# An S4D macaron block in fp32 on one core: ACT and DVE in program order from the 14th to the 49th group

## The chip, the core and the metric

One NeuronCore of a Trainium2 chip runs the whole program. The time is device microseconds (us) of one execution; lower is better. The kernel before was run three times: 1751.17 us in the median, 1746.32 and 1751.95 us at the ends.

## The reference, cut to what matters

Input x is 8 x 2048 x 256 (batch, length, channels), fp32. Three residual sublayers follow each other:

```python
x = x + 0.5 * ffn(layernorm(x), w1, b1, w2, b2)     # first half, "a"
x = x + s4d(layernorm(x), ...)                      # state-space layer, then a layer norm of its own
x = x + 0.5 * ffn(layernorm(x), w1, b1, w2, b2)     # second half, "b"

def ffn(x, w1, b1, w2, b2):
    h = relu(x @ w1 + b1)                           # 256 -> 1024
    return h @ w2 + b2                              # 1024 -> 256

def s4d(x, ...):                                    # a long convolution along the length, per channel
    K = 2 * real(sum_n Ct[h, n] * exp(dtA[h, n] * l))
    y = irfft(rfft(x, 4096) * rfft(K, 4096))[:2048]
    r = x + y + x * D
    return layernorm(r) * ln_w + ln_b
```

## The kernel before, in words

**Stages.** The convolution is made in blocks of 128 positions. It needs tables that follow from the state-space parameters alone: for every pair of channels a matrix of powers called P, and its transpose. The tables are made by the vector engines while the first FFN runs; then come the states and outputs of the convolution, then the second FFN.

**The FFN.** Every fp32 product is made of three fp32r products of high and low parts. Tokens are handled in 64 groups of 256. A group has 8 slots of the loop variable `t` in `sublayer`, one for each 128 hidden features; slot 23.4 is the fourth slot of group 23, t = 188. In a slot TensorE makes the hidden features `ph_a` (`up`, L857, six matmuls) and, three slots later (`LAG = 3`), multiplies the hidden parts `hx_a` into `po_a` (`down`, L867, six matmuls). Between them ACT makes the high part with a relu (L946) and DVE the low part (L116, `SCALAR_TENSOR_TENSOR hx_a`). PSUM holds four `ph` banks.

**Around a group.** `pre_a` loads a group (`xa`, issued from ACT's queue at L1012), takes its moments on DVE (L675, L679), normalizes on ACT (`xn`, L726), adds the bias on GpSimd (POOL, L773, pinned behind what was traced on POOL before it), turns it on TensorE (`pt_a`, L790) and splits it (ACT `xh_a` L799, DVE `xl_a` L801). `post_a` adds the result (L1023), takes moments, and writes the next layer's normalized input `u` (ACT, L726). The root and the reciprocals of a finished group are shared with a group to come: `s_u` on ACT (L686), `t_u`, `q_u`, `nb_u` on DVE (L697, L119, L708).

**The background: P.** `matrices` is a generator that `fill` advances beside the groups; each `yield` carries a pace in us that `fill` weighs against 1.32 us a slot. P is made in 32 batches:
- `make` (POOL, L599, L601, L603, L605, L607, L609): six operations of 128 x 512 into one of four areas of `u` for batches 0 to 15 (an area is used again by the batch four later), and into another set of areas for 16 to 31. L601 to L609 pass through one scratch tile, so the last four of a batch follow each other. Batch 16's scratch and area lie over tables that batches 0 to 7 read.
- `spread`: two copies on ACT (L618, `planes<-u`) split P into 16-bit halves, then SyncE's queue issues a transposing DMA (L620, `planes<-planes`) and a store (L625, `o<-u`).
- `transpose`: one copy on DVE and one on ACT (L635, `u<-planes`) put the halves together, and SyncE's queue stores them (L637, `pt<-u`). After that the area is free.

There is one buffer each for `planes` and `turned`, so the copies of a batch wait until the transposing DMA of the batch before has read them. The copies L618, L635 and the DMA L620 are pinned (`keep_in_program_order`) behind the instruction traced before them on their engine. In the program the two L618 copies of batch 6 stand in slots 21.6 and 21.7, of batch 8 in 23.4 and 23.5, of batch 9 in 24.3 and 24.4, of batch 12 in 26.7 and 27.0; the copies L635 of a batch come some 8 or 9 slots after its first L618. `lags` makes another table beside it: L535, L537, L541 on POOL, `pk` on TensorE (L549), two DVE operations, and DMAs issued by POOL (L569). The first L618 copy stands in slot 16.5, the last L635 copies in 46.2.

**What sets the order.** The program is traced in the order of the Python code. Then a scheduler orders each engine's instructions by a simulated timeline, within the data dependencies and the pins. Each engine's queue then runs in the order so fixed, and an instruction that waits holds up all behind it. `tc.manual_schedule(engines=...)` takes ACT and DVE out of the scheduler's hands for what is traced inside it: they keep the order of the code. The kernel before uses it for the slots before t = 0 alone.

Of the kernel before, what the change touches and what calls it, by code (L numbers as in the profile page):

```python
# [43 lines left out]
def macaron_s4d_kernel(  # L44
# [35 lines left out]
    XL = 8  # L80
    LAGS_BEHIND = 3
    PIN = 1
    PINF = "a1", "a2"
    MB = 1
    PINT = 1
# [23 lines left out]
    def bank(tag, name):  # L109
        return ps.tile([P, 512], F32, name=name, tag=tag, bufs=BANKS[tag])  # L110

    def slot(tag, shape, name, dtype=F32):
        return work.tile(shape, dtype, name=name, tag=tag, bufs=BUFS[tag])

    def stt(o, a, s, b, op0, op1):
        return V.scalar_tensor_tensor(out=o, in0=a, scalar=s, in1=b, op0=op0, op1=op1)  # L116
# [554 lines left out]
    def stats(srcs, name, pin=False, mv=None):  # L671
        st = stat.tile([P, NTB, 6], F32, name=f"st_{name}", tag="st")
        mv = moments(NTB, name) if mv is None else mv
        for i, src in enumerate(srcs):
            ins = V.bn_stats(st[:, i, :], src)  # L675
            if pin:
                tc.keep_in_program_order(ins)
        for i in range(NTB):
            V.bn_aggr(mv[:, i, :], st[:, i, :])  # L679
        return mv  # L680
# [64 lines left out]
    def halves(xt):  # L745
        return [xt[:, i, :] for i in range(NTB)]

    def ffn_in(xt, name, on_act=NTB, by_dma=False, joint=None, into=None):
# [7 lines left out]
        else:  # L756
            mv = stats(halves(xt), f"f{name}", name in PINF)
            yield
# [92 lines left out]
    def up(wt, xT, ph, fc):  # L851
        xh, xl = xT
        fs = slice(fc * P, (fc + 1) * P)
        n = 0
        for dc in range(NDC):
            for wp, xp in ((1, xh), (0, xl), (0, xh)):
                nc.tensor.matmul(  # L857
                    ph, wt[wp][:, dc, fs], xp[dc] if type(xp) is list else xp[:, dc, :], start=(n == 0), stop=(n == 3 * NDC - 1)
                )
                n += 1  # L860

    def down(wt, hs, po, fc):
        hh, hl = hs
        for i in range(NTB):
            tsl = slice(i * P, (i + 1) * P)
            for n, (hp, wp) in enumerate(((hl, 0), (hh, 1), (hh, 0))):
                nc.tensor.matmul(  # L867
                    po[:, i, :],
                    hp[:, tsl],
                    wt[wp][:, fc, :],  # L870
                    start=(fc == 0 and i == 0 and n == 0),
                    stop=(fc == NFC - 1 and n == 2),
                    skip_group_check=True,
                )

    def sublayer(w1t, w2t, pre, post, lead, tag, first=(), background=(), due=(), at=(), wide=None):

        xT, po, running = {}, {}, {}
        background = iter(background)
        due = dict(due)
        at = dict(at)
        now = [0.0, 0.0]
        last = {}

        def step():  # L890
            while spawned:
                key, what = spawned.pop(0)
                running["later", key] = what
            for key in list(running):
                try:
                    next(running[key])
                except StopIteration as e:
                    del running[key]
                    if key[0] == "pre":
                        xT[key[1]] = e.value  # L900

        def fill(until=None):
            while until or now[1] <= now[0]:
                pace = next(background, "end")
                if isinstance(pace, str):
                    due.pop(pace, None)
                    if pace == "end":
                        now[1] = math.inf
                    if pace in (until, "end"):
                        return  # L910
                else:
                    now[1] += pace

        W0, W1 = (wide.first, wide.end) if wide else (NG, NG)
        starts_at = {}
        for g in range(NG):
            sooner = wide.sooner(g) if wide else 0
            starts_at.setdefault(g * SLOTS - lead - sooner, []).append(g)

        ordered = ExitStack()  # L920
        if first or tag == "b" and MB:
            ordered.enter_context(
                tc.manual_schedule(engines={mybir.EngineType.Activation, mybir.EngineType.DVE})
            )
        for t in range(-lead, NG * SLOTS + LAG + 1):
            if t == 0:
                ordered.close()
            g, k, f = t // SLOTS, t % SLOTS // 2, t % 2
            if W0 <= g < W1:
                g0, fc = g // 2 * 2, (t - g // 2 * 2 * SLOTS) // 2  # L930
                if f == 0:
                    hx = wide.hidden()
                    for i in range(2):
                        pend[g0 + i, fc] = [h[:, i * TOK : (i + 1) * TOK] for h in hx]
                    ph = bank("h", f"ph_{tag}{g0}_{fc}")
                    up(w1t, wide.input(g0), ph, fc)
                    last[A_] = A_.activation(hx[0], ph, AF.Relu)  # L937
                    last[V] = stt(hx[1], ph, 0.0, hx[0].bitcast(F32), ALU.max, ALU.subtract)
            elif t >= 0 and g < NG:
                fc = 2 * k + f  # L940
                hx = slot("hx", [P, 2, TOK], f"hx_{tag}{g}_{fc}", F32R)
                hh, hl = pend[g, fc] = hx[:, 0], hx[:, 1]
                ph = bank("h", f"ph_{tag}{g}_{fc}")[:, 0:TOK]
                up(w1t, xT[g], ph, fc)

                last[A_] = A_.activation(hh, ph, AF.Relu)  # L946
                last[V] = stt(hl, ph, 0.0, hh.bitcast(F32), ALU.max, ALU.subtract)
            tb = t - LAG
            tw = t - WLAG
            if W0 * SLOTS <= tw < W1 * SLOTS:  # L950
                g0 = tw // (2 * SLOTS) * 2
                fc, i = divmod(tw - g0 * SLOTS, 2)
                if fc == 0:
                    po[g0 + i] = wide.result(f"po_{tag}{g0 + i}").rearrange("p (i m) -> p i m", i=NTB)
                down(w2t, pend.pop((g0 + i, fc)), po[g0 + i], fc)
                if fc == NFC - 1:
                    running["post", g0 + i] = post(g0 + i, po.pop(g0 + i))
            if 0 <= tb < NG * SLOTS and not W0 * SLOTS <= tb < W1 * SLOTS:
                gb, fc = tb // SLOTS, tb % SLOTS
                if tb % SLOTS == 0:  # L960
                    po[gb] = bank("o", f"po_{tag}{gb}").rearrange("p (i m) -> p i m", i=NTB)
                down(w2t, pend.pop((gb, fc)), po[gb], fc)
                for mark in [m for m, d in due.items() if d == gb]:
                    fill(mark)
                if tb % SLOTS == SLOTS - 1:
                    running["post", gb] = post(gb, po.pop(gb))
            for n in starts_at.get(t, ()):
                running["pre", n] = pre(n)
            if t == -lead:
                running["first"] = iter(first)  # L970
            step()
            if t >= 0:
                now[0] += 1.32
                with ExitStack() as behind:
                    for ins in last.values():
                        behind.enter_context(tc.issue_after(ins.ins))
                    fill()
            if t in at:
                at[t]()
        while running:  # L980
            step()
        fill("end")
# [285 lines left out]
    def begin():  # L1268
        for _ in range(sizes[1] // PB):
            next(head)  # L1270

    sublayer(
        w1t, w2t, pre_a, post_a, 19, "a", load_weights(), chain(matrices(), early()),
        {"half": NG // 2, "tables": NG * 3 // 4},
# [123 lines left out]
    def pre_b(g):  # L1398
# [8 lines left out]
        uc = [uo[:, i // CQ, :, i % CQ] for i in range(P - 1 - i0, P - 1 - i0 - NTB, -1)]  # L1407
        mv = stats(uc, f"r{g}", PIN & 2)
        yield
# [9 lines left out]
        for i in range(NTB):  # L1419
            xb = xt[:, i, :].rearrange("p (b h) -> p b h", h=BCH)  # L1420
            ins = stt(xb, uc[i], rs[:, i : i + 1], xb, ALU.mult, ALU.add)
            if PIN & 1:
                tc.keep_in_program_order(ins)
# [4 lines left out]
    def post_b(g, po):  # L1428
# [7 lines left out]
        )  # L1436

    sublayer(
        [wb1[:, i] for i in range(2)], [wb2[:, i] for i in range(2)], pre_b, post_b, 17, "b",
        wide=wide,  # L1440
# [33 lines left out]
```

## Time and profile before

| what | number |
|---|---|
| median of three runs | 1751.17 us (1746.32 to 1751.95) |
| the profiled execution | 1747.17 us, of which the span is 1745.3 us |
| busy over the span | TensorE matmul 1713.1, DVE 1368.3, ACT 968.4, POOL 586.3 us |
| mean granted TensorE clock | 0.994 |
| groups 14 to 48 | 183 to 618 us of the span |
| in these 435 us | TensorE busy 428.26, DVE 320.45, ACT 312.53, POOL 309.20 us |

In the profile PE is TensorE's matmuls and PEld its weight loads, SPq is SyncE's queue of DMA issues, and ACTq is ACT's. Times in timelines count from the start of the span. "Idle before" is the time in which an engine stood still ahead of an instruction, with what ended it.

### The profile page before, as it was taken

What the parts mean: (1) busy time and instruction counts of PE and PEld (TensorE: products, weight loads), DVE (VectorE), ACT (ScalarE), POOL (GpSimd) and SP (SyncE); (2) the same over time, 40 slices, a digit from 0 to 9 for tenths busy, and PEclk for the clock granted to TensorE, in tenths of its full rate; (3) what the DMA queues carried; (4) which work ended last, traced back from release to release, by engine and by line L of the source; (5) the groups of instructions that cost most, each with busy time, mean ns of one, the idle gap of its engine ahead of it and who ended that gap; (6) DMA issues with size and microseconds to landing.
All of it is one profiled execution on the core that took longest, in us unless ns stands there. A gap on an engine that the chain in (4) does not pass through costs nothing.

```text
span 1745.3 us, 38327 instructions
## 1 busy us (share of the span) xinstructions
PE 1713.1 (98%) x14263; PEld 1638.1 (94%) x14263; DVE 1368.3 (78%) x4591; ACT 968.4 (55%) x2040; POOL 586.3 (34%) x550
## 2 busy tenths in 40 slices
PE   9999999999999999999999899999999999999998
PEld 7999999989999999999999799999999999999998
DVE  6998776677777767766999788889888788788754
ACT  4555477677778755544555445555455455445533
POOL 1117989886776105111000132231222222222200
PEclk9999999999999999999999989999999999999999
DMA  5111166577666532236888912332223323222211
GB/s 191 47 40 53 49 178 164 160 199 205 188 167 190 134 85 68 73 91 194 263 259 260 292 49 72 70 90 56 67 73 73 73 67 79 73 67 73 63 48 37
DMA packets 276849, 204.24 MB, mean 117 GB/s; under 512 B 162740, under 2 KB 235188, under 8 KB 276150
## 3 DMA queue, kind: packets, MB, share of 16 engines
q1 hardware_dynamic: 249232, 168.08, 36.2%
q10 hardware_dynamic: 26502, 32.52, 5.9%
q8 instruction: 112, 1.84, 0.4%
q0 software_dynamic: 928, 1.19, 0.3%
q14 instruction: 75, 0.61, 0.1%
HBM read 91.89 MB, written 71.57 MB: 94 GB/s over the span
## 4 chain that ended last, share of the span: by engine, by line
PE 80%; DVE 12%; DMA 4%; issue 1%; ACT 1%; SPq 0%; POOL 0%; ACTq 0%; DVEq 0%
PE po_b L867 21%; PE ph_b L857 20%; PE po_a L867 19%; PE ph_a L857 18%; DVE e L1160 2%; DMA planes<-planes 2%; DVE te L1161 2%; DVE xsB L1163 1%; DVE xsA L1163 1%; PE pt_a L790 1%; DVE xsA L1162 1%; DVE xsB L1162 1%; DMA xa<-in_L_attn_x_dram 1%; DMA wb<-w_dram 1%; PE pv L1130 1%
## 5 line engine op out<-in xcount | busy, mean ns | idle before, releaser
L867 PE MATMUL po_a<-wa,hx_a 128*128 128x256 f32 x3072 | 454.7, 285 | 6.8 <-DVE hx_a L116 6.6
L857 PE MATMUL ph_a<-xh_a,wa 128*128 128x256 f32 x2048 | 456.4, 287 | 1.2 <-ACT xh_a L799 0.7
L867 PEld LDWEIGHTS po_a<-wa,hx_a 128*128 128x128 f32 x3072 | 405.3, 192 | 9.5 <-DVE hx_a L116 8.0
L857 PEld LDWEIGHTS ph_a<-xh_a,wa 128*128 128x128 f32 x2048 | 355.3, 193 | 4.3 <-ACT wa L194 1.5
L946 ACT ACTIVATE hx_a<-ph_a 128x256 fp32r<-128x256 f32 x512 | 193.8, 388 | 229.5 <-PE ph_a L857 207.4
L116 DVE SCALAR_TENSOR_TENSOR hx_a<-ph_a,hx_a 128x256 fp32r<-128x256 f32 x512 | 209.0, 414 | 121.8 <-ACT hx_a L946 119.8
L867 PEld LDWEIGHTS po_b<-wb,hb 128*128 128x128 f32 x2208 | 288.1, 191 | 14.4
L867 PE MATMUL po_b<-wb,hb 128*128 128x256 f32 x2208 | 292.6, 282 | 0.0
L857 PE MATMUL ph_a<-xl_a,wa 128*128 128x256 f32 x1024 | 290.3, 285 | 0.0
L857 PE MATMUL ph_b<-xh_b,wb 128*128 128x256 f32 (+1 forms) x928 | 249.8, 327 | 0.7 <-ACT xh_b L799 0.7
L937 ACT ACTIVATE hb<-ph_b 128x512 fp32r<-128x512 f32 x184 | 109.2, 594 | 162.1 <-PE ph_b L857 161.2
L857 PEld LDWEIGHTS ph_a<-xl_a,wa 128*128 128x128 f32 x1024 | 197.4, 193 | 0.6 <-DVE xl_a L801 0.4
L116 DVE SCALAR_TENSOR_TENSOR hb<-ph_b,hb 128x512 fp32r<-128x512 f32 x184 | 124.9, 679 | 83.3 <-ACT hb L937 81.0
L773 POOL TENSOR_TENSOR xa<-xa,hb 128x512 f32<-128x512 f32 x64 | 85.1, 1330 | 286.9 <-ACT xn L726 245.9
L857 PEld LDWEIGHTS ph_b<-xh_b,wb 128*128 128x128 f32 x928 | 167.3, 193 | 12.8 <-ACT xh_b L799 1.1
L857 PE MATMUL ph_b<-xl_b,wb 128*128 128x256 f32 (+1 forms) x464 | 151.1, 327 | 0.0
L857 PE MATMUL ph_b<-even,wb 128*128 128x512 f32 x576 | 149.0, 393 | 0.0
L867 PE MATMUL po_b<-wb,hx_b 128*128 128x256 f32 x864 | 126.5, 285 | 3.9 <-DVE hx_b L116 3.9
L867 PEld LDWEIGHTS po_b<-wb,hx_b 128*128 128x128 f32 x864 | 114.2, 193 | 4.8 <-DVE hx_b L116 4.5
L857 PEld LDWEIGHTS ph_b<-even,wb 128*128 128x128 f32 x576 | 102.4, 189 | 16.9
L773 POOL TENSOR_TENSOR u<-u,hb 128x512 f32<-128x512 f32 x32 | 46.4, 1449 | 177.0 <-ACT xn L726 144.6
L946 ACT ACTIVATE hx_b<-ph_b 128x256 fp32r<-128x256 f32 x144 | 54.0, 381 | 73.0 <-PE ph_b L857 67.9
(292 smaller groups left out, 3028.4 us busy)
## 6 DMA issues: line engine op xcount, KB each, us to landing
o<-u SPq DMA_DIRECT2D x32, 512.0 KB, 4.0
pt<-u SPq DMA_DIRECT2D x32, 512.0 KB, 4.0
tz<-kpad SPq DMA_DIRECT2D x64, 256.0 KB, 4.5
x_dram<-xa ACTq DMA_DIRECT2D x62, 256.0 KB, 2.1
xa<-in_L_attn_x_dram ACTq DMA_DIRECT2D x61, 256.0 KB, 3.0
pt<-pt SPq DMA_DIRECT2D x60, 256.0 KB, 3.7
ot<-o SPq DMA_DIRECT2D x48, 256.0 KB, 4.1
u<-x_dram SPq DMA_DIRECT2D x32, 256.0 KB, 2.8
```

The source lines that it names most:

```text
L116: return V.scalar_tensor_tensor(out=o, in0=a, scalar=s, in1=b, op0=op0, op1=op1)
L773: return G_.tensor_add(xt, xt, hb2.unsqueeze(1).to_broadcast([P, NTB, H]))
L790: nc.tensor.transpose(pt[:, dc * TOK + i * P : dc * TOK + (i + 1) * P], xn[:, i, dc * P : (dc + 1) * P], ident,)
L857: nc.tensor.matmul(ph, wt[wp][:, dc, fs], xp[dc] if type(xp) is list else xp[:, dc, :], start=(n == 0), stop=(n == 3 * NDC - 1))
L867: nc.tensor.matmul(po[:, i, :], hp[:, tsl], wt[wp][:, fc, :], start=(fc == 0 and i == 0 and n == 0), stop=(fc == NFC - 1 and n == 2), skip ...
L937: last[A_] = A_.activation(hx[0], ph, AF.Relu)
L946: last[A_] = A_.activation(hh, ph, AF.Relu)
L1130: ins = nc.tensor.matmul(pv[ri][c * N : (c + 1) * N, l, j0 * B : j1 * B], pts[c][:, l, ri * N : (ri + 1) * N], some(j0, j1)[:, :, BCH * bt ...
L1160: E.tensor_mul(t1, xv[:, :, :, j, :], wr_b)
L1161: E.tensor_mul(t2, xv[:, ::-1, :, j, :], wi_b)
L1162: E.tensor_add(xv[:, :, :, j + 1, :], xv[:, :, :, j + 1, :], t1)
L1163: E.tensor_add(xv[:, :, :, j + 1, :], xv[:, :, :, j + 1, :], t2)
```

## The change

Two places: a pair of slots, and a block in the loop of `sublayer` that opens `manual_schedule` for ACT and DVE at the start of the 14th group of the first FFN and closes it at the start of the 49th. What lies inside, the background included, keeps the order of the code on these two engines. No instruction is added, removed or altered; POOL, TensorE and SyncE stay with the scheduler.

```diff
@@ -80,6 +80,7 @@
     PIN = 1
+    IN_ORDER = 14 * 8, 49 * 8
     PINF = "a1", "a2"
@@ -925,6 +926,14 @@
         for t in range(-lead, NG * SLOTS + LAG + 1):
             if t == 0:
                 ordered.close()
+
+            if tag == "a" and t in IN_ORDER:
+                if t == IN_ORDER[0]:
+                    ordered.enter_context(
+                        tc.manual_schedule(engines={mybir.EngineType.Activation, mybir.EngineType.DVE})
+                    )
+                else:
+                    ordered.close()
             g, k, f = t // SLOTS, t % SLOTS // 2, t % 2
```

## The prediction

> **What bounds the kernel now.** First the page: the busy shares, and the rows of its slices for TensorE, POOL and the clock (a slice is 43.6 us).
>
> ```profile
> PE 1713.1 (98%) x14263; PEld 1638.1 (94%) x14263; DVE 1368.3 (78%) x4591; ACT 968.4 (55%) x2040; POOL 586.3 (34%) x550
> PE   9999999999999999999999899999999999999998
> POOL 1117989886776105111000132231222222222200
> ```
>
> TensorE bounds the program, so the change is worth what it does to TensorE's idle time between 183 and 618 us, where groups 14 to 48 lie. POOL is busy 80 to 90% in the slices from 175 to 400 us: there P is made. Next, busy time by stretches of 10 us (columns: PE, PEld, DVE, ACT, POOL, clock, DMA share, GB/s):
>
> ```profile
> 325.00:335.00 10.00, 10.00 (x88) 10.00 (x87) 5.40 (x21) 4.71 (x10) 9.37 (x9) 1.00 0.52 122
> 335.00:345.00 10.00, 8.15 (x56) 7.95 (x55) 6.61 (x18) 7.14 (x12) 3.17 (x3) 0.83 0.63 194
> 345.00:355.00 10.00, 9.08 (x75) 8.84 (x74) 5.66 (x20) 7.00 (x13) 9.99 (x11) 1.00 0.91 209
> 385.00:395.00 10.00, 7.14 (x60) 6.94 (x59) 6.96 (x27) 6.88 (x13) 8.69 (x8) 1.00 1.10 283
> ```
>
> All the loss sits in a few stretches: 56 matmuls instead of 86 to 88, then 75, then 60. TensorE's idle time before single instructions from 183 to 618 us is 1.85 us at 340.10, 0.92 at 354.83, 0.36 at 356.88, 2.86 at 392.93 and 0.56 at 563.67; with some shorter gaps 6.74 us. In the clock record one period of 3.41 us from 340.14 us stands at 0.5, which is 1.7 us of work. Together 8.4 us: more than this the change can't bring. Then the timelines of the three engines around the first stall:
>
> ```profile
> 327.44 1.99 ACT L618 COPY planes<-u 128x1024 uint16<-128x1024 uint16 x2
> 332.09 0.38 ACT L946 ACTIVATE hx_a<-ph_a 128x256 fp32r<-128x256 f32 x1 [1.31 <-PE ph_a L857]
> 336.13 1.99 ACT L618 COPY planes<-u 128x1024 uint16<-128x1024 uint16 x2 [3.65 <-DMA planes<-planes]
> ...
> 332.85 0.17 DVE L708 RECIPROCAL t_u<-q_u 128x4 f32<-128x4 f32 x1
> 336.15 1.30 DVE L635 COPY u<-planes 128x1024 uint16<-128x1024 uint16 x1 [3.13 <-DMA planes<-planes]
> ...
> 337.97 0.28 PE L857 MATMUL ph_a<-xh_a,wa 128*128 128x256 f32 x1
> 340.10 1.65 PE L867 MATMUL po_a<-wa,hx_a 128*128 128x256 f32 x6 [1.85 <-DVE hx_a L116]
> ```
>
> The copies at 327.44 are batch 8's, those at 336.13 batch 9's. Between them lie 8.7 us, and batch 8's transposing DMA took 6.6 us of these (329.45 to 336.0). Both engines stand at the front of their queues for that DMA, with relus and low parts behind them; TensorE runs dry. In the code the two batches' copies are seven slots apart. They came so close because batch 8 was late: its copies follow the relu of slot 23.4, which ended at 305.70, and 32 later instructions of ACT were let past them. POOL shows why:
>
> ```profile
> 289.77 1.06 POOL L599 TENSOR_TENSOR u<-u 128x512 f32<-128x512 f32 x1 [2.03 <-DVE mv_j L679]
> 290.79 1.06 POOL L605 TENSOR_TENSOR u<-u 128x512 f32<-128x512 f32 x1
> 291.81 1.28 POOL L609 TENSOR_TENSOR u<-u 128x512 f32<-128x512 f32 x1
> ...
> 296.81 1.28 POOL L609 TENSOR_TENSOR u<-u 128x512 f32<-128x512 f32 x1
> ...
> 322.11 1.29 POOL L609 TENSOR_TENSOR u<-u 128x512 f32<-128x512 f32 x1
> ```
>
> L609 ends a batch: 6 at 293.1, 7 at 298.1, 8 only at 323.4. At 289.77 POOL starts batch 9 before it has ended batch 6, and idles for that. Between 298.1 and 323.4 it does batch 8's last four operations (4.9 us), all that is left of batch 16 (6.0), L541, L535 and L537 (4.6), three bias additions (3.9), the starts of batches 10 and 11 (4.2) and DMA issues (2.1).
>
> **The change part by part.** No operation changes; what moves is the order. I laid the trace's rows against the code. Of ACT's instructions from group 32 to 48, 63 of 331 stand elsewhere than in the code, by at most four places, and TensorE idles 0.56 us there: for ACT the order of the code nearly ran there already. In groups 22 to 31 it is 179 of 194, up to 32 places. So ACT's change falls between 270 and 410 us. On DVE most instructions move by a few places everywhere.
>
> *TensorE's cushion.* A slot is six `ph` and six `po` matmuls, 0.72 us each six. From the end of `ph` of a slot to the `po` that needs its `hx` lie three of each, 4.3 us. The relu (0.38), the low part (0.41) and two handovers of 0.1 take 0.9 or 1.0 of it. ACT or DVE may be 3.4 us late at no cost; beyond that TensorE waits one for one, once, since all later slots shift with it.
>
> *What goes: up to 8.4 us.* The stalls at 340, 355 and 393 us come from batches that crowd. In the code's order they stay seven slots (10 us) apart, more than one DMA (median 4.7, longest 7.5 us from issue to landing) and its copies. The 8.4 us can go.
>
> *What comes: ACT waits for POOL.* Copies that are not ready now hold up ACT itself: queued behind them are the relus, and DVE's low parts and TensorE wait for those. The price is how late L609 is behind the relu ahead of the copies, less 3.4 us. POOL can't keep its order: what needs a copy that stands behind the waiting one can't run ahead of it any more.
> - Batch 6: the relu of slot 21.6 ended at 281.10. L607 of batch 6 ended at 287.7. Batch 9's start needs the area of batch 5, whose L635 copies stand in slot 22.0, behind the waiting ones, so it can't come in between; L609 then ends at 289.0 or sooner. That is 289.0 - 281.1 - 3.4 = 4.5 us at most. Without batch 8's start (2.1) and L535, L537 (1.2), which the code has later, it is 285.7, and 1.2 us.
> - Batch 8: 305.7 + 3.4 = 309.1. POOL free at 298.1, own four operations 4.9, one bias addition 1.3: 304.3, no stall. If all of the trace's work stays in between except what can't (batch 11's start and the bias of group 25, 3.4 us), L609 ends at 320.0: 10.9 us.
> I take 2.0 us for both together, 1.2 to 10.9. It is nearer the lower end, because the rows of batches 7, 9 and 10 show the last four operations back to back, about 5 us, and what was done for batch 6 or 8 is a stall paid once.
>
> *What comes: bursts.* In the order of the code each relu waits for all of the slot before. I added the slots' work on ACT and DVE by start-to-start distances (relu 0.27, low part 0.33, `planes` copy 0.95, `u` 0.65 us) against 1.44 us a slot: one place exceeds the cushion, group 15, by 0.5 us (table work beside 13 small operations of `q_u`, `nb_u`). Taken by full durations, which overlap in the trace, the same sum gives far more, so I keep 0 to 3 us, and take 0.5: groups 32 to 48 lose next to nothing.
>
> *DVE's copies beside POOL.* L635 on DVE took 0.73 to 3.12 us, on ACT 1.32 to 1.42. At its worst 2.4 us over the shortest, it stays under the cushion: nothing. The Trainium skill (SBUF — State Buffer, "Who interferes with whom") says that a DVE copy in a two-port mode and a GpSimd operation exclude each other for a whole instruction, which speaks against a fixed order on DVE beside a busy POOL. By that page the excess is one POOL operation, an estimate of 1.3 us, again nothing in the sum.
>
> *The clock.* An idle gap of 1.85 us came with a period of 3.41 us at half clock, one of 2.86 us with none. So a new stall costs 0 or 1.7 us more; I take 0. The Trainium skill (TensorE: Matmul & The Clock Gate, "What's actually happening") has the clock fall after an idle window of about 3.4 us, free-running; by that alone no stall of 2 us would pay, and the row at 340 shows one that did.
>
> Outside the stretch the order is the scheduler's again; I put it at nothing, as TensorE hides it there as before (98%).
>
> Sum: 8.4 - 2.0 - 0.5 = 5.9 us less. The profiled execution took 1747.17 us (span 1745.3 and 1.9 around it), 4.0 under the median of the runs; against the median 1751.2 - 5.9 = 1745.3 us. The forecast's own ends: 8.4 less, or 8.4 - 4.5 - 3.0 = 0.9 less: 1742.8 to 1750.3.
>
> **The rivals.**
> - *Slower: POOL becomes the bound.* One place, batch 8: if POOL still does batch 16 and the rest first, ACT stands 10.9 us. It decides as soon as that batch's L609 ends later than 305.7 + 3.4 + 8.4 = 317.5 on the trace's scale. Later batches add at most what is left of batch 12's lateness (L609 at 369.8, the relu ahead of it at 349.9): 369.8 - 349.9 - 10.9 - 3.4 = 5.6. With 0.5 for bursts and 1.7 for the clock, 10.9 + 5.6 + 2.2 - 8.4 = 10.3 us more, 1761.5. For: POOL is busy 90% from 200 to 340 us. Against: much of that is work for later batches, and an ACT that waits serves POOL's results at once instead of 4 us after.
> - *No change: the loss moves.* Batches 6 and 8 together cost 5 to 8 us, in place of the crowding: 8.4 - 6.5 - 0.5 = 1.4 us less, 1749.8. For: POOL has the same work. Against: its idle time ahead of batch 9 (2.03 us) goes.
>
> **How the numbers follow.** What a measurement of this kernel can tell from no change is 0.3%, 5.3 us. The forecast gets 0.45, the slower rival 0.28, the other 0.27. The range goes from 1739, as single runs lie 5 us under the median, to 1762, the slower rival's sum; outside I leave some 0.15.
>
> **What would show it.** Right: no gap of PE at `po_a` over 1 us between 330 and 400 us, L618 copies seven slots apart and their waits on POOL (L609) rather than on the DMA, 2 to 5 us in all; PE busy 432 of 435 us. Wrong: ACT idle for 10 us or more before `planes` L618 with L609 as the releaser, relus behind it, PE idle there; or gaps at low parts spread over all groups, which would be the bursts.

## The result: slower by 1.4%

The changed kernel took 1774.78 us in the median of four runs (1773.86 to 1780.26), the kernel before 1751.56 us beside it: ratio 1.0144, 95% interval 1.0123 to 1.0165. The prediction was 1745.3 us, with a range from 1739 to 1762. It was wrong in sign.

The page of the changed kernel's profile (span 1773.3 us, before 1745.3), busy shares and the slices of TensorE and POOL:

```profile
PE 1722.3 (97%) x14263; PEld 1643.3 (93%) x14263; DVE 1375.0 (78%) x4591; ACT 965.8 (54%) x2040; POOL 586.0 (33%) x550
PE   9999999899999999999999979999999999999998
POOL 1117988974676113211000032231222222222210
```

The work is the same; the span is 28.0 us longer. Where these 28.0 us were lost is read best by laying the two traces beside each other, slot by slot. For the first slot of each group I take the start of the relu, after less before, and how much that grows from one group to a later one. TensorE's idle time and the time lost at half clock in the same groups stand beside it (both us; a half-clock period of 3.4 us counts as 1.7):

| groups | growth | TensorE idle, before → after | lost at half clock, before → after |
|---|---|---|---|
| 14 to 20 | +7.1 | 0.0 → 4.7 | 0.0 → 1.7 |
| 20 to 33 | +12.0 | 6.2 → 14.3 | 1.7 → 6.8 |
| 33 to 42 | +0.1 | 0.0 → 0.0 | 0.0 → 0.0 |
| 42 to 50 | +11.4 | 0.6 → 7.7 | 0.0 → 0.0 |
| 50 to the end | -2.7 | | |

So there are three losses, and a calm stretch in which the order of the code costs nothing at all. Stretches of the changed kernel, columns as in the prediction (PE, PEld, DVE, ACT, POOL, clock, DMA share, GB/s):

```profile
205.00:215.00 10.00, 6.05 (x38) 5.85 (x38) 8.51 (x21) 2.06 (x6) 9.04 (x11) 0.83 0.10 29
320.00:330.00 10.00, 7.78 (x52) 7.79 (x53) 7.40 (x29) 8.38 (x16) 9.84 (x12) 0.83 0.87 201
335.00:345.00 10.00, 6.40 (x35) 6.40 (x36) 5.47 (x21) 6.76 (x13) 9.45 (x9) 0.66 0.61 170
560.00:570.00 10.00, 7.64 (x63) 7.29 (x62) 8.23 (x31) 6.44 (x13) 7.94 (x7) 1.00 0.47 105
```

Before, a slice of 10 us lost its matmuls in three places only, all after 335 us; now it does so at 210 us already (38 matmuls of some 86), again around 322, 338 and 375, and at 566 us without any half clock.

**First loss, group 15.** The timeline of the changed kernel, three engines (start, length, engine, line):

```profile
204.26 1.33 POOL L774 TENSOR_TENSOR xa<-xa,hb 128x512 f32<-128x512 f32 x1
...
208.56 1.08 POOL L606 TENSOR_TENSOR u<-u 128x512 f32<-128x512 f32 x1
209.80 0.63 POOL L538 TENSOR_TENSOR u<-u 128x256 f32<-128x256 f32 x1 [0.16 <-DVE u L525]
...
204.41 5.45 DVE L525 TENSOR_SCALAR u<-u 128x128 f32<-128x128 f32 x2
209.78 1.07 DVE L117 SCALAR_TENSOR_TENSOR hx_a<-ph_a,hx_a 128x256 fp32r<-128x256 f32 x3
...
210.24 1.42 PE L868 MATMUL po_a<-wa,hx_a 128*128 128x256 f32 x6 [3.94 <-DVE hx_a L117]
```

And the same place before:

```profile
203.51 2.23 DVE L524 TENSOR_SCALAR u<-u 128x128 f32<-128x128 f32 x2
...
204.21 1.32 POOL L773 TENSOR_TENSOR xa<-xa,hb 128x512 f32<-128x512 f32 x1
205.69 0.63 POOL L537 TENSOR_TENSOR u<-u 128x256 f32<-128x256 f32 x1 [0.17 <-DVE u L524]
```

L525 negates two small tables for `lags` (lines are one higher than before, nine higher after the new block). One of the two took 5.31 us, until 209.72. POOL had run without a gap from 203.24 to 209.64, one operation starting before the last had ended. Three low parts queued behind it, and TensorE idled 3.94 us. Before, the same instruction took 2.10 us and ended at 205.61: there POOL had a gap after L773, at 205.53. In both kernels the gap stands where POOL waits for this very instruction, ahead of L538 (L537 before). Before, that place came right behind the bias addition; in the change four operations of P stood between.

**Second loss, groups 20 to 33.** Timeline of ACT and TensorE:

```profile
281.81 1.04 ACT L619 COPY planes<-u 128x1024 uint16<-128x1024 uint16 x1 [4.57 <-DMA planes<-planes]
...
320.38 1.04 ACT L619 COPY planes<-u 128x1024 uint16<-128x1024 uint16 x1 [6.10 <-POOL u L610]
336.76 1.04 ACT L619 COPY planes<-u 128x1024 uint16<-128x1024 uint16 x1 [7.61 <-POOL u L610]
...
283.67 0.33 PE L791 MATMUL pt_a<-ident,xn 128*128 128x128 f32 x1 [2.54 <-ACT xn L727]
322.22 0.98 PE L868 MATMUL po_a<-wa,hx_a 128*128 128x256 f32 x6 [2.60 <-DVE hx_a L117]
338.60 1.65 PE L868 MATMUL po_a<-wa,hx_a 128*128 128x256 f32 x6 [4.12 <-DVE hx_a L117]
```

ACT stands in front of a `planes` copy with the relus behind it. Behind the two waits for POOL, TensorE idles for what the wait exceeds its cushion. Behind the first one it idles more than that, 2.54 us for a wait of 4.57, since there it waits for `xn` and not for a low part. The list of waits from 183 to 660 us (engine, line, what ended the wait, us in all, times, longest) has two releasers where the prediction had one:

```profile
DVE hx_a L117 <- ACT hx_a L955: 132.4, 118, 6.7
ACT planes L619 <- DMA planes<-planes: 30.3, 14, 5.7
ACT planes L619 <- POOL u L610: 14.6, 3, 7.6
```

Before, these were 74.6, 17.6 and 1.3 us. For ACT the larger releaser is the transposing DMA of the batch before. For TensorE, in groups 20 to 33, it is POOL: 6.7 us idle and 5.1 at half clock stand at the two long waits for L610, 5.5 us idle (2.54, 2.19 at 374.67, 0.79 at 388.28) and 1.7 at half clock at waits for the DMA.

**Third loss, groups 42 to 49.** From group 44 on a group is turned by a DMA instead of on TensorE (`DMA_A = 44`), and the first of these is prepared from slot 42.1 on. DVE's timeline at the largest of its stalls, and TensorE's:

```profile
563.68 0.75 DVE L676 BATCH_NORM_STATS2 st_u<-xa 128x6 f32<-128x256 f32 x2
564.35 0.30 DVE L680 BATCH_NORM_AGGREGATE mv_j<-st_u 128x2 f32<-128x6 f32 x2
564.57 1.36 DVE L636 COPY u<-planes 128x1024 uint16<-128x1024 uint16 x1
565.83 0.40 DVE L117 SCALAR_TENSOR_TENSOR hx_a<-ph_a,hx_a 128x256 fp32r<-128x256 f32 x1
...
566.29 0.98 PE L868 MATMUL po_a<-wa,hx_a 128*128 128x256 f32 x6 [2.36 <-DVE hx_a L117]
```

ACT had waited 2.33 us for the DMA just before (its copy at 558.51), so DVE's slot 42.2 began late; and there the moments, the sum of `post_a` and now P's copy L636 stand in one row, 3.7 us from 562.10 to 565.8, ahead of the low part of slot 42.3.

### The profile page after: what moved, and what is told of

Its sections match the earlier page's. It is cut to its first block, busy times and chain, and to the rows that moved or that the text cites. A ratio compares the mean times of both kernels' runs of the same rounds, so it can differ in the third digit from the quotient of the medians.

```text
span 1773.3 us, 38322 instructions
## 1 busy us (share of the span) xinstructions
PE 1722.3 (97%) x14263; PEld 1643.3 (93%) x14263; DVE 1375.0 (78%) x4591; ACT 965.8 (54%) x2040; POOL 586.0 (33%) x550
## 4 chain that ended last, share of the span: by engine, by line
PE 80%; DVE 9%; DMA 4%; ACT 3%; issue 2%; POOL 1%; ACTq 0%; SPq 0%; DVEq 0%; POOLq 0%
PE po_b L868 20%; PE ph_b L858 19%; PE ph_a L858 16%; PE po_a L868 16%; DMA planes<-planes 3%; PE py L1214 3%; PE py L1205 3%; PE pv L1139 2%; DVE hx_a L117 1%; PE pt_a L791 1%; ACT hx_a L955 1%; ACT planes L619 1%; ACT xn L727 1%; DMA pt<-pt 1%; DVE e L1169 1%
## 5 line engine op out<-in xcount | busy, mean ns | idle before, releaser
L868 PE MATMUL po_a<-wa,hx_a 128*128 128x256 f32 x3072 | 459.5, 287 | 21.0 <-DVE hx_a L117 20.5
L868 PEld LDWEIGHTS po_b<-wb,hb 128*128 128x128 f32 x2208 | 288.1, 191 | 14.4
L858 PEld LDWEIGHTS ph_b<-xh_b,wb 128*128 128x128 f32 x928 | 167.3, 193 | 12.8 <-ACT xh_b L800 1.1
L858 PEld LDWEIGHTS ph_b<-xl_b,wb 128*128 128x128 f32 x464 | 89.6, 193 | 4.1 <-DVE xl_b L842 0.3
```

The lines of the kernel that those rows point to most:

```text
L858: nc.tensor.matmul(ph, wt[wp][:, dc, fs], xp[dc] if type(xp) is list else xp[:, dc, :], start=(n == 0), stop=(n == 3 * NDC - 1))
L868: nc.tensor.matmul(po[:, i, :], hp[:, tsl], wt[wp][:, fc, :], start=(fc == 0 and i == 0 and n == 0), stop=(fc == NFC - 1 and n == 2), skip ...
```

## Experiments

The table uses the same measure: the growth in us by groups, each kernel's profiled execution against the one of before. Where the change leaves groups 20 to 33 to the scheduler (e4, e9, e13) they still came out 2.3 to 4.3 us longer, with up to 3.4 us of it at half clock. So a difference under some 4 us in that stretch is not read. The same holds, with some 3 us, from group 42 on: e12 and e13 leave ACT and DVE to the scheduler from there to group 47 in nearly the same order as before, and came out 2.9 and 3.1 us longer. e15 and e16 ran 12 times, e17 six times, the others once. "Beside" is the kernel before on the same chip.

| kernel | 14 to 20 | 20 to 33 | 33 to 42 | 42 to 50 | us | beside |
|---|---|---|---|---|---|---|
| the change | +7.1 | +12.0 | +0.1 | +11.4 | 1774.78 | 1751.56 |
| e1_act_only | +1.9 | +9.4 | +4.5 | +7.6 | 1767.83 | 1749.60 |
| e2_dve_only | +5.5 | +3.6 | +1.9 | +9.3 | 1765.65 | 1749.60 |
| e3_14_to_42 | +8.1 | +9.8 | +0.4 | +5.2 | 1772.36 | 1749.60 |
| e4_42_to_49 | 0.0 | +3.6 | +0.6 | +9.2 | 1759.46 | 1749.60 |
| e5_negate_on_act | +0.4 | +12.7 | +0.9 | +9.7 | 1771.00 | 1751.87 |
| e6_pool_too | +0.6 | +6.4 | +1.8 | +8.3 | 1768.06 | 1751.87 |
| e7_slower_pace | +3.8 | +0.1 | +6.4 | +17.9 | 1772.05 | 1751.87 |
| e8_dma_a_step_sooner | +7.3 | +3.8 | +9.8 | +8.6 | 1780.42 | 1751.87 |
| e9_late_shift | 0.0 | +4.3 | 0.0 | +8.0 | 1757.84 | 1755.21 |
| e10_four_engines | +0.6 | +8.0 | +0.3 | +10.7 | 1767.01 | 1755.21 |
| e11_four_and_pace | +1.9 | -6.8 | 0.0 | +11.0 | 1751.93 | 1755.21 |
| e12_pool_alone | +0.4 | -0.7 | +0.1 | +2.9 | 1750.07 | 1755.21 |
| e13_48_to_56 | +0.1 | +2.3 | 0.0 | +5.6 | 1754.92 | 1752.22 |
| e14_no_dma_turn | +8.2 | +13.2 | +1.5 | +8.2 | 1782.84 | 1752.22 |
| e15_four_to_42 | +1.9 | -7.2 | 0.0 | +7.1 | 1749.58 | 1752.22 |
| e16_slow_then_fast | +1.9 | -6.4 | +3.5 | +7.3 | 1754.02 | 1751.97 |
| e17_pool_alone_act | 0.0 | +0.3 | +9.7 | +11.7 | 1765.13 | 1751.18 |

### One engine alone: e1, e2

```diff
-  tc.manual_schedule(engines={mybir.EngineType.Activation, mybir.EngineType.DVE})
+  tc.manual_schedule(engines={mybir.EngineType.Activation})     # e1
+  tc.manual_schedule(engines={mybir.EngineType.DVE})            # e2
```

> ACT alone keeps the order of the code from group 14 to 49; DVE is the scheduler's. Theory A (ACT's queue: the copies L618 stand in it for POOL and for the transposing DMA, relus behind): most of the loss stays, span 15 to 25 us above before, with ACT idle before L618 of 30 us or more in groups 16 to 30 and again in groups 42 to 45. Theory D (DVE's queue: low parts held by bursts and by blocked DVE instructions): within 5 us of before.

> DVE alone keeps the order of the code from group 14 to 49; ACT is the scheduler's. Theory D: 12 to 25 us above before, the step of 5 us at group 15 included (the DVE instruction of 5.3 us). Theory A: within 5 us of before, apart from that step.

Neither theory holds alone: the times lie 18.2 and 16.1 us above the one beside them, where the theory of the other engine allowed 5 us. The step at group 15 comes with DVE's order (L525 took 5.31 us in e2, 2.25 in e1). The middle loss comes mostly with ACT's order: 9.4 us, with 17.5 us of waits for L610 and 17.0 for the DMA; with DVE's order 3.6 us, which is no more than runs differ by. The late loss comes with either, 7.6 and 9.3 us.

### One stretch alone: e3, e4

```diff
-    IN_ORDER = 14 * 8, 49 * 8
+    IN_ORDER = 14 * 8, 42 * 8      # e3
+    IN_ORDER = 42 * 8, 49 * 8      # e4
```

> Both engines, but closed at group 42 instead of 49. If the losses before and after group 42 are separate, the relu of group 42 comes 19 us later than before, as with the change, and the 11.5 us that the change lost from group 42 to 49 go: span 15 to 20 us above before. If the late loss is a consequence of the early delay, it stays at 25 to 31 us.

> Both engines, groups 42 to 49 alone. Separate losses: nothing changes before group 42, then 9 to 13 us are lost by group 49. If the late loss needs the early delay: under 3 us.

The late loss is a loss of its own: 9.2 us in e4, where nothing was late when it began. In e3, where the scheduler ordered those groups, 5.2 us were lost there, of which some 3 are not read; its time, 22.8 us above the one beside it, lies between the two ranges.

### The blocked instruction: e5

```diff
-                V.tensor_scalar_mul(v, v, -1.0)
+                A_.activation(v, v, AF.Copy, scale=-1.0)
```

> The change, with one thing altered: the two negations of 128 x 128 (L525, tensor_scalar_mul by -1) run on ACT instead of DVE, at the same place in the code. Theory 'a DVE operation is shut out by POOL' (in the profile after, one of them took 5.32 us in slot 15.3, until POOL's row of operations had its first gap): the step of 5.1 us at group 16 goes to under 1 us, the later losses stay, 1768 to 1771 us. Rival 'burst' (slot 15.3 holds too much work for DVE, whatever runs on POOL): DVE loses only the 2 us that such an operation takes elsewhere, a step of 3 us or more stays, 1772 to 1775.

The step is gone (-0.1 us at group 16), the other losses are as they were, 1771.0 us: the theory that POOL shuts the DVE operation out holds, and the rival, that slot 15.3 holds too much work, falls. On ACT the two took 0.50 us together.

### POOL and SyncE in order too: e6, e10

```diff
-  engines={mybir.EngineType.Activation, mybir.EngineType.DVE}
+  engines={mybir.EngineType.Activation, mybir.EngineType.DVE, mybir.EngineType.Pool}                      # e6
+  engines={mybir.EngineType.Activation, mybir.EngineType.DVE, mybir.EngineType.Pool, mybir.EngineType.SP} # e10
```

> The change, with POOL kept in the order of the code too, for the same groups. Theory 'POOL works out of step' (it starts later batches and tables before the last operations of the batch that ACT waits for): ACT's waits for L610, 14.6 us in the profile after, fall below 4 us, groups 20 to 33 lose 5 to 8 us less, 1766 to 1770. Rival 'POOL has too little time' (the code gives a batch fewer slots than POOL needs with all else that it does there): the waits stay at 10 us or more, 1772 to 1782.

> The change, with POOL and SyncE's queue in the order of the code too. In e6_pool_too POOL's order took away the step at group 16 and most of the waits for L610. Theory 'the code's places leave the transposing DMA too little time': SyncE issued it within 0.1 us of its last copy in the profile after, so its order matters little; groups 20 to 33 lose 5 to 7 us, 42 to 49 about 10, 1765 to 1770. Rival 'other stores ahead of it in SyncE's queue': the waits for the DMA, 25.5 us in e6_pool_too, fall under 15 and the time under 1764.

In e6 the waits from 183 to 660 us were these; POOL's L610 is down from 14.6 to 1.3 us, and with the 3.4 us for L542 to 4.7:

```profile
ACT planes L619 <- DMA planes<-planes: 25.5, 15, 6.4
ACT planes L619 <- POOL u L542: 3.4, 1, 3.4
ACT planes L619 <- POOL u L610: 1.3, 1, 1.3
```

So it was POOL's order and not its speed: kept in step it has the batches ready, and the time, 1768.06 us, is where that theory put it. The middle loss fell by 5.6 us, from 12.0 to 6.4; nearly all of that, 5.1, is time at half clock that went with the two longest stalls; TensorE's idle time fell by only 2.2 us, from 14.3 to 12.1. What it did not remove are the waits for the DMA, and a new one came, which is the blocked instruction again. Timeline of e6:

```profile
314.60 5.27 DVE L636 COPY u<-planes 128x1024 uint16<-128x1024 uint16 x1
...
314.64 1.30 POOL L610 TENSOR_TENSOR u<-u 128x512 f32<-128x512 f32 x1
...
318.22 1.04 POOL L602 TENSOR_TENSOR u<-u 128x512 f32<-128x512 f32 x1
319.35 1.07 POOL L542 TENSOR_TENSOR u<-u 64x256 f32<-64x256 f32 x1
...
320.22 0.98 PE L868 MATMUL po_a<-wa,hx_a 128*128 128x256 f32 x6 [2.62 <-DVE hx_a L117]
```

A copy that takes 0.72 us elsewhere took 5.27. POOL's operations follow each other without a gap from 314.64 to 319.26 (318.22 + 1.04); there 0.09 us are free, and the copy ends 0.6 us after. SyncE's order (e10) changed nothing: 27.5 us of waits for the DMA, 8.0 us lost in the middle. The DMA was issued within 0.1 us of its last copy with or without it.

### Where the copies stand: e7, e8

```diff
-                now[0] += 1.32
+                now[0] += 1.24 if tag == "a" and t >= 14 * 8 else 1.32                 # e7, held to group 50
```

```diff
             for w in range(2):
                 tc.keep_in_program_order(A_.copy(planes[:, w], pu[:, w]))
-                yield
+            yield                                                                      # e8
...
-            for _ in range(4):                                                         # in transpose
+            for _ in range(3):
```

> The change, with a slot counted as 1.24 us instead of 1.32 us from group 14 on, so that each batch of P takes 6% more slots (the last copies stand in 48.2 instead of 46.2; the fixed order is held to group 50). Theory 'the code's places are too tight' (ACT stands in front of copies whose POOL result or transposing DMA isn't there yet): waits before L619 fall from 45 us to under 20, groups 20 to 49 lose under 12 us instead of 25, 1757 to 1764 with the step at group 16 still there. Rival 'bursts' (ACT and DVE in the order of the code can't keep up with a slot, whenever the copies come): the loss stays within 4 us of the change's, 1771 to 1779.

> The change, with both L619 copies of a batch in one step of the background (at the place of the first) and the L636 copies and the transposing DMA a step sooner, so that the DMA has five steps instead of four (about 8 us instead of 6.6) before the next batch's copies. Theory 'the DMA lands too late': ACT's waits for it before L619, 30.1 us in the profile after, fall below 12 us, and the groups from 20 on lose 5 to 10 us less, 1764 to 1770. Rival 'POOL sets the pace': the waits for L610 grow by what those for the DMA lose, 1772 to 1778.

Both took most of the middle loss away (+0.1 and +3.8 us from 20 to 33, where the change lost 12.0) and both lost it again later, so neither total came out as its theory had it: e8 lies above both its ranges, e7 in that of its rival. In e8 the waits for the DMA fell from 30.3 to 12.8 us as expected, those for POOL from 14.6 to 5.9, against the rival; but the L636 copies, a step sooner, now met slots 2 and 3 from group 33 on, and 9.8 us went there where the change lost 0.1. That this is the cause is not shown: two transposing DMAs were also issued 1.6 us late there. In e7 the waits of over 0.8 us before L619 fell from 34.7 to 14.4 us in groups 20 to 33, but all of them from 183 to 660 us hardly, from 46.1 to 42.3. Later, six transposing DMAs were issued 1.2 to 3.9 us late, 13.4 us together, each right after the store L626 of a later batch, which SyncE's queue held ahead of it. I take this for the cause of its late loss, and not its rival's bursts; e11 below bears on it.

### The late loss: e9, e13, e14

```diff
-                now[0] += 1.32
+                now[0] += 0.0 if tag == "a" and t in (42 * 8, 42 * 8 + 1) else 1.32    # e9, with IN_ORDER = 42 * 8, 49 * 8
-    IN_ORDER = 14 * 8, 49 * 8
+    IN_ORDER = 48 * 8, 56 * 8                                                          # e13
-    DMA_A = 44
+    DMA_A = 64                                                                         # e14
```

> ACT and DVE in the order of the code for groups 42 to 48 alone (as in e4_42_to_49, which lost 9.2 us from the first slot of group 42 on), with the background held back two slots at the start of group 42, so that the L619 copies stand in slots 2 and 3 instead of 0 and 1 and the L636 copies in slot 4 instead of 2, away from the moments and the sum of post_a. Theory 'the copies stand beside the burst of slot 2': less than 4 us lost from group 42 on, 1750 to 1755 in all. Rival 'the transposing DMA': its distance to the next copies is the same five slots, so 7 to 10 us are lost again, 1757 to 1761.

> ACT and DVE in the order of the code for groups 48 to 55 alone, where nothing of P is made any more (its last copies stand in slot 46.2) and every group is turned by DMA. Theory 'the bursts of the groups that are turned by DMA' (moments, reciprocals and splits in slots 2 to 7, 9.0 us of DVE's queue in six slots of 1.44 us): about 1 us a group is lost, 5 to 9 us from group 48 to 56, 1755 to 1762 in all. Rival 'they lose only where P's copies stand between them': under 2.5 us, within 2 us of the kernel before beside it.

> The change, with every group of the first FFN turned on TensorE (DMA_A 64 instead of 44), which is some 0.4 us more of TensorE's work in each group from 44 on. The late loss begins in slot 42.1, where the first groups to be turned by DMA are prepared. Theory 'turning by DMA makes the burst': groups 42 to 49 lose under 4 us against the kernel before (11.4 in the profile after), some 2 of it transposes. Rival 'P's copies and the transposing DMA of P': 8 us or more are lost there as before. The time in all isn't to be compared: all later groups pay for the transposes.

In e9 the loss of group 42 fell from 4.5 to 2.2 us as the copies left slot 2, which is less than is read here, and group 43 to 49 lost as before: 8.0 in all. So the place in slot 2 explains a quarter at most. The rival's price came true and its reason didn't: no `planes` copy of these groups waited for the DMA for 0.8 us or more. In e13, with the groups turned by DMA but nothing of P, the order of the code cost 1.2 us over eight groups (5.7 at group 48, 6.9 at 56): the theory of the bursts alone falls. In e14, with P and without the turning by DMA, the loss was 8.2 us. Transposes on TensorE cost 0.47 us a group there (3.8 us from group 55 to 63), so 2.8 for six groups; of the 5.4 left, 4.5 stand in group 42, at the same stall as in the change (2.39 us idle, here with 1.7 at half clock), and 0.9 after. By the bare 8.2 the rival's "8 or more" is met, by what is left without the transposes neither range. I read it so: group 42's part belongs to P's copies, and the larger part after it (6.5 us in the change) needs both, as neither e13 nor e14 lost it. Why is only argued. In the changed kernel's group 43 DVE's row from the moments to the splits, with one P copy in it, took 9.1 us (575.48 to 584.56), 0.73 of it idle; six slots of 1.44 us are 8.6. That leaves little slack in which a delay of ACT or DVE could be made good.

### Kernels made from these findings: e11, e15, e16, e12, e17

```diff
+  engines={mybir.EngineType.Activation, mybir.EngineType.DVE, mybir.EngineType.Pool, mybir.EngineType.SP} # e11, e15, e16
+                now[0] += 1.24 if tag == "a" and t >= 14 * 8 else 1.32                 # e11 (to group 50), e15 (to group 42)
+                now[0] += 1.32 if tag != "a" or t < 14 * 8 else 1.24 if t < 32 * 8 else 1.45   # e16 (to group 42)
+  engines={mybir.EngineType.Pool}                                                      # e12, e17
+        P_REINT = (A_.copy, A_.copy)                                                   # e17
```

> ACT, DVE, POOL and SyncE's queue in the order of the code, and a slot counted as 1.24 us (held to group 50). In e7_slower_pace the slower pace alone took the loss of groups 20 to 33 away (0.1 us instead of 12.0), but a late loss of 24 us stood after group 36, where SyncE issued six transposing DMAs 1.2 to 3.9 us late behind a later batch's store. Theory 'lateness of POOL and of SyncE's queue behind copies in a fixed order': no step at group 16, under 3 us from 20 to 33, no late issues, under 12 us after 36: 1752 to 1762. Rival 'a slower pace puts the copies on the bursts': the late loss stays over 18 us, 1768 to 1775.

> ACT, DVE, POOL and SyncE's queue in the order of the code for groups 14 to 41 with a slot counted as 1.24 us, and the scheduler's order from group 42 on. In e11_four_and_pace the slots of groups 20 to 42 gained 4.9 us on the kernel before and those of 42 to 49 lost 11. Theory 'the order of the code costs nothing where no copy is late, and loses only in the groups that are turned by DMA': 1745 to 1750, ratio 0.995 to 0.999. Rival 'the loss comes with P's late end' (its copies now reach to slot 48.2, whoever orders them): 1752 to 1758, ratio over 1.

> As e15_four_to_42 (ACT, DVE, POOL and SyncE's queue in the order of the code for groups 14 to 41, the scheduler from group 42), but a slot counts as 1.24 us only up to group 31 and as 1.45 us after, when POOL has time, so that the last copies of P stand in 45.7 instead of 48.2. e15 had gained 5.1 us on the kernel before by group 42 and lost 7.5 from there to group 49, where P met the groups that are turned by DMA. Theory 'the late loss is P's work beside these groups': most of the gain stays, 1744 to 1749, ratio 0.994 to 0.998. Rival 'a faster pace brings the late copies back': the seven-slot batches after group 32 wait for POOL and the transposing DMA again, 1750 to 1756, ratio 0.9985 or more.

> POOL alone in the order of the code for groups 14 to 48; ACT, DVE and SyncE are the scheduler's, as before. My prediction put the stalls of the kernel before at 340 to 393 us down to POOL ending batch 8 late (L609 at 323.4). If that is so, L610 of batch 8 ends before 312 us, the copies of batches 8 and 9 stand seven slots apart, and the stretch loses 3 to 8 us less than before: 1743 to 1749 against 1750 to 1752 beside it. Rival 'the scheduler needs POOL's freedom': POOL waits for buffers in its order and the time is 1751 to 1758.

> POOL alone in the order of the code for groups 14 to 48 (as in e12_pool_alone), and both L636 copies of a batch on ACT instead of one on DVE and one on ACT. In e12 one L636 copy took 5.66 us on DVE (0.7 us where POOL is idle), from the start of POOL's row of operations to a handover in it, and TensorE idled 3.3 us after it with 3.4 us at half clock. Theory 'POOL's row shuts a DVE copy out': no such stall, groups 20 to 33 gain 3 to 6 us on e12, 1743 to 1748, ratio 0.994 to 0.998. Rival 'ACT gets too much' (another 32 x 1.35 us in its queue, relus behind them): stalls of relus take its place, 1750 to 1757.

e11 decides the main question. With all four engines in the order of the code and the background at a slower pace, groups 20 to 33 ran 6.8 us faster than before. The stretch from 185 to 430 us, in this order: before, the change, e11:

```profile
185.00:430.00 245.00, 238.82 (x1975) 236.97 (x1974) 175.77 (x634) 168.50 (x322) 207.63 (x195) 0.99 0.58 163
185.00:430.00 245.00, 225.94 (x1814) 222.94 (x1813) 167.31 (x584) 153.27 (x295) 199.14 (x188) 0.97 0.55 153
185.00:430.00 245.00, 241.96 (x2016) 240.04 (x2015) 178.64 (x652) 170.74 (x328) 199.82 (x192) 1.00 0.56 154
```

TensorE is busy 242 of 245 us there, and the clock never falls. The order of the code isn't bad for ACT and DVE there; what was bad is that it made ACT stand for what POOL and the DMA had not brought. ACT's waits before L619 fell from 46.1 us in the change to 21.6 (14.5 for the DMA, 2.7 for POOL). Neither half does it alone: four engines at the old pace still lost 8.0 us in the middle (e10), and the slower pace alone came out level there (+0.1) and lost its time later (e7). No transposing DMA was issued late in e11. The late loss stayed, 11.0 us, and brings it to 1751.93 us, just under what that theory gave, against a single 1755.21 beside it.

e15 gives groups 42 to 49 back to the scheduler: 1749.58 us in the median of 12 runs, ratio 0.9985 (0.9973 to 0.9996). That is faster than both kernels, by less than what is told from no change here (0.3%). The time is where its theory put it. But only half of the theory's reason is borne out: e15 kept the 7.2 us of the middle and lost 7.1 after group 42 all the same, most of it in group 44, under the scheduler's order. The rival's reason was that P now ends in slot 48.2. e16 ends P in slot 45.7, by a faster pace after group 32, and lost as much after group 42, 7.3 us; so P's late end alone does not explain it, and the cause stays open. In time e16's rival came true: waits came back from group 33 on (3.5 us lost; one wait of 3.17 us for the DMA at 35.7), ratio 1.0015 (1.0004 to 1.0026).

e12 tests what the prediction said of the kernel before. With POOL alone in order, L610 of batch 8 ended at 299.0 instead of 323.4, the copies of batches 8 and 9 stood 17.7 us apart instead of 8.7, and the stalls at 340 and 393 us were gone; batch 12, ahead of the second, ended at 343.0 instead of 369.8. So both came with POOL's order and its late batches. But one L636 copy, blocked for 5.66 us, cost a stall of 3.29 us and a half-clock period instead; from 20 to 33 only 0.7 us was won, which is no more than runs differ by, and the time, 1750.07 us, lies between the two ranges. e17 takes that copy off DVE: no DVE operation over 1.8 us is left in these groups, and yet it is 0.75% slower (ratio 1.0075, 1.0055 to 1.0095). The rival was right in kind, and the price was higher than its 1757: with 32 more copies on ACT, DVE's waits for relus grew (114.7 us from 183 to 660 us, 79.6 in e12), and 9.7 us went from group 33 to 42.

## Why the prediction was wrong, by its steps

- *The cushion of 3.4 us: right.* ACT's waits of 6.10 and 7.61 us for L610 became idle gaps of 2.60 and 4.12 us; less 3.4 they would be 2.7 and 4.2. It holds for the path through the low parts alone: where TensorE waited for `xn`, a wait of 4.57 us left 2.54, and the sum had no such path.
- *"The 8.4 us can go": right in kind and nearly in size,* 6.8 in e11 and 7.2 in e15. In the change itself none of it shows.
- *"They stay seven slots (10 us) apart, more than one DMA ... and its copies": the step that failed, with the next one, in the middle.* I measured the distance from one batch's copies to the next. But the DMA isn't issued with the copies: it overwrites `turned`, so it waits for the L636 copies of the batch before, which stand two or three slots later. In the change the last of these ended at 274.7, the DMA was issued at once, and it landed at 281.7, 7.0 us later; ACT had been in front of the next L619 since 277.2. ACT stood 30.3 us for this DMA, twice as long as for POOL, and TensorE lost 5.5 us idle and 1.7 at half clock at these waits in groups 20 to 33. The sum had no term for them.
- *ACT waits for POOL, taken at 2.0 us: mis-sized.* Batch 6 cost nothing, batch 8 2.6 us and batch 9 4.1 us of idle TensorE, 6.7 in all, with 5.1 more at half clock at both places. The slower rival named this wait rightly but not its price or place: counted on the trace of before, batch 8's L610 ended at 309.9 (320.3 less the 10.4 by which group 23 was already late), before its 317.5. The argument against it, that a waiting ACT serves POOL at once, did not help: the long waits for L610 went only where POOL itself was put in step (e6, e10, e11).
- *Bursts 0.5 us, "groups 32 to 48 lose next to nothing": right from 33 to 42 (0.1 us), wrong from 42 on (11.4).* My sum by start-to-start distances took the slots one by one, with relus on time. It missed that the L636 copies drift into slot 2, and that groups turned by DMA, with P's copies among them, leave DVE little slack from slot 2 to slot 7. That a delay is then passed back and forth between the two engines is my reading, not shown by itself; DVE's waits for a relu rose from 74.6 to 132.4 us from 183 to 660 us. I had also taken it for a good sign that ACT's instructions stand at most four places from the code's order there; ACT's order alone (e1) still lost 7.6 us from group 42 on.
- *DVE's operations beside POOL, "nothing": wrong.* The step cost 3.94 us of idle time and 1.7 at half clock. I had bounded it by the L635 copies of the trace (3.12 us at most) and not looked at L524, which had its gap in POOL's row only because the scheduler had put POOL's own wait for it there. The Trainium skill (SBUF — State Buffer, "Who interferes with whom") speaks of an exclusive lock on the shared port pair. The rows agree that the two exclude each other; but here DVE did not wait for one POOL operation, as my estimate of 1.3 us had it: L525 waited while five of them ended. The copies mostly did wait for one (below).
- *The clock, taken at 0 us: 6.8 us.* Five periods of 3.4 us came in the place of one. Which stall brings one is not set by its length alone: 2.60 us at 322 had one, 2.54 at 284 and 2.36 at 566 had none, and the last one's like in e5 (2.4 us at 562) had. The Trainium skill (TensorE: Matmul & The Clock Gate, "What's actually happening") has the clock fall after an idle window of about 3.4 us, free-running. That a like stall falls now in one, now not, fits a free-running window; that stalls of 2.60 and 2.19 us (at 374.67) sufficed does not fit a whole idle one.
- *Of the 28.0 us in the profiles, some 4 are the starting point:* the profiled execution of before, 1747.17 us, lay 4.4 us under the median of its runs. The medians differ by 23.2 us.

What stays open: how the 6 to 7 us from group 43 to 49 divide between ACT and DVE, since either order alone (e1, e2) brought most of it; and why e15 and e16 lost 7 us after group 42 under the scheduler's order, where e12 and e13 lost 3.

## What to carry to other kernels

Before an engine is fixed to the order of the code, list for each instruction in it that can wait every producer, and measure the distance from where the producer can really start (here a DMA that waits for the reader of its buffer) to the place of the wait. Where that is shorter than the producer takes, all behind it pays whatever exceeds the cushion; fix the producers' queues too, and move the waiting instruction later, rather than only the waiting engine. A DVE operation that a row of POOL's can hold up, as L525 here, is safest where POOL's row has a gap, or on ACT if ACT has room (it had for L525 in e5, not for the L636 copies in e17).

## What the runs showed of the hardware beyond what I expected

- A DVE operation from SBUF to SBUF can be held by several POOL operations that follow each other without a gap: 5.31 us (L525 in the change), 5.27 and 5.66 us (L636 in e6 and e12), each ending within some 0.6 us of POOL's first gap, even one of 0.09 us. But that is the exception. Of 23 L636 copies of the change that met a running POOL operation, 22 ended 0.6 to 0.7 us after the end of that one, six of them though POOL went straight on; the other one waited for two. What lets a copy in at one handover and not at another the runs do not show.
- An interruption of TensorE costs more than the idle time that the profile shows: the last matmul before it is shown 0.28 us long, where the next one otherwise starts 0.12 us later, and the first after it is followed only 0.22 us later. That is 0.26 us a gap; with 14 gaps from group 42 to 50 it is 3.6 us, and the idle time there was 7.7.
